# A two-layer graph network on one core: features in place and between the first ticks, the order check later, x over two queues

## The chip, the core and the metric

The kernel runs on one core of a Trainium2 chip. The core has a matrix engine (TensorE, PE in the profile, with its weight loads as PEld), a vector engine (VectorE, DVE), a scalar engine (ScalarE, ACT), a general engine (GpSimd, POOL) and a queue engine (SyncE, SP). Each takes its own instructions in order; they meet through semaphores. DMA transfers are issued by SP, ACT or POOL and run beside the engines. The metric is the device time of one execution in microseconds, as a median of several runs.

## The reference, cut to what matters

There are N = 12500 nodes with 64 features and E = 200000 edges from `src` to `dst`, with `dst` sorted. Two blocks follow each other, both with a residual:

```
h  = relu(layernorm(x))
h1 = relu(mean over edges into v of h[src]  @ W1l.T + b1 + h  @ W1r.T)
x2 = x + (mean over edges into v of h1[src] @ W2l.T + b2 + h1 @ W2r.T)

h  = relu(layernorm(x2))
m  = relu(concat(h[src], h[dst], edge_attr) @ LW1 + lb1) @ LW2 + lb2
out = x2 + mean of m over the edges that leave v
```

The two means of the first block are called the first and the second convolution below; the second block is the message stage.

## The kernel before, in words

**Blocks and cells.** The nodes are cut into 49 blocks of 256 (128 partitions, two nodes each). The edges of one block of destinations are a window of `dst`; within it they are sorted by the block of their source into 49 cells of up to 128 edges. So there are 49 x 49 = 2401 cells. A convolution goes through all cells in order, four at a time; one such step is called a tick below. For a cell PE gathers source features with a one-hot matrix (`got`, L890), ACT copies them to SBUF as bf16 (`rows`, L894), and PE adds them up by destination with a second one-hot matrix (`acc`, L769). DVE makes the one-hot matrices: `turned` (L735) from the row `srow`, two halves for each part of 16 cells, and `hot` (L744) from columns, one for each tick. Features are kept as three bf16 terms whose sum is the f32 number: table `ta` for the first convolution, `tb` for the second.

**Sorting.** `sort(B)` (L589 to L663) ranks the edges of block B on DVE, PE and ACT. It writes the rows `srow_b`, `srow_k` and `drow_k` to DRAM and columns to SBUF; it has 13 steps. `srow` is loaded back from `srow_b`, one part at a time, two parts ahead (L725). `edges_in` loads `src` and `dst` of the next blocks (`ids_i`, L545), from places in `begin_i`, which `find_blocks` has computed.

**The block search.** `find_blocks` (L18 to L109) loads all of `dst` as 125 rows of 1600 (`find_d`), checks that `dst` is in order (L33 to L42, L105 to L109: each number against its neighbour, with two small loads `find_n` for the neighbours at the ends of rows), shifts the numbers to block numbers (L47, L50) and counts where each block begins. The iota `find_ids_i` (L53) is made by POOL, behind the copy `seen` (L699), which waits for the last chunk of x, and the clearing of the end of `tb` (L700). `bad` gets 1 where the fast path can't be used; it is copied to `which` (L959) when the first convolution has been written out in the program, and a general path runs at the end if it is 1.

**Features.** x is loaded into the space of `tb` in seven chunks of seven blocks, by ACT's queue (L203, L208). `features` (L470 to L497) makes `ta` from them: for each chunk two reductions, a subtraction of the mean, a reciprocal and a multiplication on DVE (`layernorm_relu`, L325 to L338), Square, Sqrt, Relu and two copies on ACT, two subtractions on POOL (L348, L352). Its scratch (`h1`, `ln_sq`, `three_r` and statistics) is in a pool of its own, "in". The chunks are begun one after the other, two ticks of a `Line` apart, each tick one step of every chunk under way. After each tick `others` makes two steps of the block search, one of the sorter and one of the clearing. Only when all seven chunks, the search and the first block's sort are written out do the pools of the first convolution open.

**Clearing.** The tables `terms` in DRAM must be zero before edge terms are scattered into them. `zeros` (L272 to L284) issues one such transfer of zeros at each call, on SP: 52 for the first four tables (48 of 640 KB), then smaller ones for the others. In the first convolution a call is made for so many cells as the generator says (5 for the first four tables).

**Beside the convolutions.** From cell 150 on `edge_terms` (L357 to L427) multiplies edge features with weights, and POOL scatters them into `terms` (L385).

**What sets the order.** The program is written in the order in which it is to be run: each generator's step appends its instructions to the engines' queues, and each engine works them off in that order.

## Time and profile before

| what | value |
| --- | --- |
| three runs, median | 3682.99 us (3680.9 to 3687.05) |
| profiled execution | 3679.43 us |
| its span | 3677.6 us |
| granted clock of TensorE, mean | 0.988 |
| first `turned` of the first convolution | 89.7 us |
| last instructions of the first convolution, `which` copied | 1307.4 us |
| DVE instructions L735, L744 in the whole span | 777.6 + 320.2 us and 807.5 us |
| POOL scatters L385 | 1904.0 us, 1666 of 1143 ns |

The page gives, for each engine, busy time and share of the span. A window gives the same for a stretch. In a timeline a row is the start in us, the length in us, engine, line, operation, output and inputs; in square brackets is how long the engine had stood idle before it and what ended that. In the chain of waits each step is what released the one after it; "issue" is time in which the engine waited for nothing that the profile shows. SPq, ACTq and DVEq are the engines' queues, with the DMAs that they issue.

### The profile page before, as it was taken

Reading aid. Unit: us, or ns where it says so; the run is one execution under the profiler, and the core shown is the slowest. Engines: PE = TensorE matmul, PEld = TensorE weight load, DVE = VectorE, ACT = ScalarE, POOL = GpSimd, SP = SyncE. Lnnn points to the kernel's source line nnn. Section 1 sums busy time; section 2 is a strip of 40 time slices with the busy share of each in tenths; the row PEclk is TensorE's granted clock in tenths of the full one; section 3 lists DMA queues with packets and bytes.
Section 4 is the critical chain, followed back from the end, with each engine's and each line's share of the span. In section 5 each row is a group of like instructions: output and inputs, shape, how many; then the busy total and the mean of one; then the engine's idle time right before and its main releaser. Section 6 shows DMA issues by size and latency. Waiting matters only on the chain.

```text
span 3677.6 us, 126942 instructions
## 1 busy us (share of the span) xinstructions
PE 3425.8 (93%) x50925; PEld 3367.7 (92%) x50925; DVE 3269.0 (89%) x5738; ACT 2506.9 (68%) x5949; POOL 2698.3 (73%) x2305
## 2 busy tenths in 40 slices
PE   1799999999899999999999998999999999999987
PEld 0788989898889999999999997999999999999887
DVE  7999999999999978788788787899889998998998
ACT  3455656565556667777777775788888888887665
POOL 4067787777777877777777773788888888887444
PEclk9999999999999999999999999999999999999999
DMA  6754545554454434444444444666766666666664
GB/s 211 268 164 150 169 152 163 155 161 151 147 168 145 128 125 142 132 137 147 136 131 137 140 134 144 224 214 200 218 212 211 204 214 214 207 207 206 194 211 140
DMA packets 413671, 635.66 MB, mean 173 GB/s; under 512 B 94131, under 2 KB 296247, under 8 KB 413070
## 3 DMA queue, kind: packets, MB, share of 16 engines
q1 hardware_dynamic: 353106, 572.87, 49.4%
q0 software_dynamic: 53312, 51.36, 4.1%
q8 instruction: 399, 6.54, 0.7%
q10 hardware_dynamic: 6652, 3.24, 0.4%
q14 instruction: 202, 1.65, 0.1%
HBM read 474.72 MB, written 155.83 MB: 171 GB/s over the span
## 4 chain that ended last, share of the span: by engine, by line
PE 64%; DVE 25%; DMA 5%; issue 3%; POOL 2%; SPq 1%; ACT 1%; DVEq 0%; ACTq 0%; POOLq 0%
PE acc L769 23%; PE got L890 13%; PE got L1071 12%; PE got L1072 6%; DVE hot L744 6%; DVE turned L735 4%; PE pE L417 3%; DVE hot_r L629 3%; PE pE L402 2%; DVE ranks L617 1%; DVE turned_d L735 1%; POOL terms L385 1%; DMA terms<-tb 1%; DMA terms_in<-terms 1%; DVE hot L594 1%
## 5 line engine op out<-in xcount | busy, mean ns | idle before, releaser
L385 POOL DMA_INDIRECT terms<-terms_o,turn_i x1666 | 1904.0, 1143 | 649.9 <-issue 427.8
L894 ACT CAST rows<-got 128x384 bf16<-128x384 f32 x2402 | 1038.4, 485 | 657.2 <-PE got L890 642.6
L769 PEld LDWEIGHTS <-hot 128*128 128x128 bf16 x12006 | 1032.5, 99 | 13.5 <-issue 4.0
L769 PE MATMUL acc<-rows,hot 128*128 128x193 bf16 x9604 | 1010.8, 248 | 0.0
L1083 POOL TENSOR_TENSOR hidden<-hidden 128x512 f32<-128x512 f32 (+1 forms) x602 | 756.4, 1256 | 265.1 <-ACT hidden L1080 179.5
L890 PEld LDWEIGHTS <-turned 128*128 128x128 bf16 x9604 | 814.6, 98 | 88.1 <-DVE turned L735 58.9
L744 DVE TENSOR_TENSOR hot<-dcol,local 128x1024 bf16<-128x1024 bf16 x1202 | 807.5, 682 | 9.0 <-PE acc L769 8.1
L735 DVE TENSOR_SCALAR turned<-srow,nid 128x2048 bf16<-128x2048 bf16 (+1 forms) x906 | 777.6, 872 | 20.7 <-issue 10.6
L1071 PE MATMUL got<-ta,turned 128*128 128x128 bf16 x3920 | 600.1, 221 | 7.3 <-DVE turned L735 7.3
L1071 PE MATMUL got<-tb,turned_d 128*128 128x128 bf16 x3920 | 600.6, 221 | 1.1 <-DVE turned_d L735 0.8
L890 PE MATMUL got<-ta,turned 128*128 128x192 bf16 x4802 | 510.5, 249 | 71.5 <-DVE turned L735 47.9
L1072 PE MATMUL got<-tb,turned_d 128*128 128x64 bf16 x3920 | 546.3, 193 | 0.0
L1072 PE MATMUL got<-ta,turned 128*128 128x64 bf16 x3920 | 546.1, 193 | 0.0
L1091 ACT ACTIVATE hot_a<-every,scol 128x256 bf16<-128x256 bf16 x1200 | 507.0, 493 | 0.0
L890 PE MATMUL got<-tb,turned 128*128 128x192 bf16 x4802 | 494.4, 246 | 0.9 <-DVE turned L735 0.5
L1080 ACT ACTIVATE hidden<-y 128x512 f32<-128x512 f32 (+1 forms) x301 | 190.4, 633 | 272.5 <-DVE y L1077 156.2
L1071 PEld LDWEIGHTS <-turned 128*128 128x128 bf16 x3920 | 362.1, 98 | 8.2 <-issue 7.8
L1071 PEld LDWEIGHTS <-turned_d 128*128 128x128 bf16 x3920 | 359.5, 98 | 1.7 <-DVE turned_d L735 1.7
L1072 PEld LDWEIGHTS <-turned 128*128 128x128 bf16 x3920 | 359.4, 98 | 1.2
L1072 PEld LDWEIGHTS <-turned_d 128*128 128x128 bf16 x3920 | 359.9, 98 | 0.0
L1093 ACT ACTIVATE hot_a<-hot_a 128x1024 bf16<-128x1024 bf16 x300 | 317.2, 1057 | 9.5
L735 DVE TENSOR_SCALAR turned_d<-drow,nid 128x2048 bf16<-128x2048 bf16 (+2 forms) x302 | 320.2, 1101 | 0.0
(217 smaller groups left out, 4898.1 us busy)
## 6 DMA issues: line engine op xcount, KB each, us to landing
srow<-srow_b SPq DMA_DIRECT2D x300, 512.0 KB
srow<-srow_k SPq DMA_DIRECT2D x149, 512.0 KB
drow<-drow_k SPq DMA_DIRECT2D x149, 512.0 KB
terms_in<-terms SPq DMA_DIRECT2D x294, 160.0 KB
edges<-in_edge_attr_dram SPq DMA_DIRECT2D x200, 192.0 KB
terms<-tb SPq DMA_DIRECT2D x200, 160.0 KB
terms<-tb SPq DMA_DIRECT2D x48, 640.0 KB
terms<-terms_o,turn_i POOLq DMA_INDIRECT x1666
```

Of the source, the lines that this page charges most:

```text
L385: nc.gpsimd.indirect_dma_start(out=terms[j][:], out_offset=bass.IndirectOffsetOnAxis(ap=at[:, c, h:h + 1], axis=0), in_=o[:, c, h], in_off ...
L735: nc.vector.tensor_scalar(o[:, h, :n * S], r[:, :n * S], nid[:, h:h + 1], None, op0=OP.is_equal)
L744: nc.vector.tensor_tensor(o[:, :n], cols.rearrange("p (g c) -> p g c", c=2).unsqueeze(2).to_broadcast([P, n, 2 * P, 2]), local.rearrange(" ...
L769: nc.tensor.matmul(self.acc[B][:, h, :W3], lt, r[:, c, 0:W3], start=k + h == 0, stop=k == row - 1 and h == 1, skip_group_check=True)
L890: nc.tensor.matmul(p[:, (i - c) * D3:(i - c + 1) * D3], t[:, h, (a - c0 + i) * S:(a - c0 + i + 1) * S], table[:, (a + i) % NB, h], start=h ...
L894: nc.scalar.copy(g[:, c:c + m, :D3], p[:, :m * D3].rearrange("p (c d) -> p c d", c=m))
L1071: nc.tensor.matmul(p[:, c], lt, rt[:, 0:2 * D], start=i == 0, stop=False, skip_group_check=True)
L1072: nc.tensor.matmul(p[:, c, 0:D], lt, rt[:, 2 * D:], start=False, stop=i == 3, skip_group_check=True)
L1080: nc.scalar.activation(w[:, :n, 0:D], y[:, :n], AF.Relu)
L1083: nc.gpsimd.tensor_sub(w[:, :n, (i + 1) * D:(i + 2) * D], w[:, :n, j], upper(w)[:, :n, j])
L1091: nc.scalar.activation(q[:, c - k], every, AF.Abs, scale=-1.0, bias=scol[:, scol_at[last] + a + c:scol_at[last] + a + c + 1])
L1093: nc.scalar.activation(q[:, :n - k], q[:, :n - k], AF.Relu, bias=1.0, scale=-2.0)
```

## The change

1. `features` works in place: the chunk itself (in the space of `tb`) takes mean, scale, Relu and the remainder of the first term, and the scratch for squares and statistics is a buffer named `edges` of the pool "terms", which is used for edge features only later. The pool "in" is gone.
2. `features` is a generator. The loop ahead of the first convolution ends as soon as the search is done, the first block is sorted and chunk 0 is finished. What is left of the other chunks is taken up between the ticks of the first convolution: one step of the line at each tick, and more where the cells five ahead need a chunk that isn't finished.
3. The order check leaves `find_blocks`. `order_check` loads `dst` again, once more as rows of 1600 with one number of the next row behind, and compares in the first ticks of the second convolution; `which` is copied after it.
4. Of the seven chunks of x the first two are loaded by ACT, the other five by SP, right behind `find_d`.

The diff, with lines of no weight left out:

```diff
@@ find_blocks
-    n = work.tile([R, 2], I32, name="find_n")
-    rows = dst.rearrange("(r c) -> r c", c=C)
-    nc.vector.memset(n, 0)
-    nc.sync.dma_start(n[0:R - 1, 0:1], rows[0:R - 1, C - 1:C])
-    nc.sync.dma_start(n[0:R - 1, 1:2], rows[1:R, 0:1])
     yield
-    down = work.tile([R, C], BF, name="find_down")
-    nc.vector.tensor_tensor(down[:, 0:C - 1], d[:, 0:C - 1], d[:, 1:C], op=OP.is_gt)
-    nc.vector.tensor_tensor(down[:, C - 1:C], n[:, 0:1], n[:, 1:2], op=OP.is_gt)
+    nc.vector.tensor_scalar(d, d, blk.bit_length() - 1, None, op0=OP.arith_shift_right)
     yield
-    flags = work.tile([R, 1], FT, name="find_flags")
-    nc.vector.tensor_reduce(flags, down, AX.X, OP.max)
-    yield
-    q = d
-    nc.vector.tensor_scalar(q, d, blk.bit_length() - 1, None, op0=OP.arith_shift_right)
-    yield
-    qb = down
-    nc.vector.tensor_copy(qb, q)
+    q = work.tile([R, C], BF, name="find_q")
+    nc.vector.tensor_copy(q, d)
+    first = work.tile([R, 1], FT, name="find_first")
+    nc.vector.tensor_copy(first, d[:, 0:1])
...
-    pf = psum.tile([1, P], FT, name="find_pf")
-    nc.tensor.transpose(pf[:, :R], flags, ident[:R, :R])
+
+def order_check(tc, work, psum, ident, bad, dst):
+    nc = tc.nc
+    R = 125
+    C = dst.shape[0] // R
+    rows = dst.rearrange("(r c) -> r c", c=C)
+    d = work.tile([R, C + 1], I32, name="order_d")
+    nc.vector.memset(d[96:R, C:], 2 ** 30)
+    nc.sync.dma_start(d[:, 0:C], rows)
+    nc.sync.dma_start(d[0:R - 1, C:], rows[1:R, 0:1])
+    for _ in range(4):
+        yield
+    down = work.tile([R, C], BF, name="order_down")
+    nc.vector.tensor_tensor(down[:, 0:C // 2], d[:, 0:C // 2], d[:, 1:C // 2 + 1], op=OP.is_gt)
     yield
-    f = work.tile([1, 1], FT, name="find_f")
-    nc.vector.tensor_reduce(f, pf[:, :R], AX.X, OP.max)
+    nc.vector.tensor_tensor(down[:, C // 2:], d[:, C // 2:C], d[:, C // 2 + 1:], op=OP.is_gt)
+    yield
+    for k in (C // 2, C // 4):
+        nc.vector.tensor_max(down[:, 0:k], down[:, 0:k], down[:, k:2 * k])
+    yield
+    flags = work.tile([R, 1], FT, name="order_flags")
+    nc.vector.tensor_reduce(flags, down[:, 0:C // 4], AX.X, OP.max)
+    yield
+    p = psum.tile([P, 512], FT, name="pX")
+    nc.tensor.transpose(p[0:1, :R], flags, ident[:R, :R])
+    yield
+    f = work.tile([1, 1], FT, name="order_f")
+    nc.vector.tensor_reduce(f, p[0:1, :R], AX.X, OP.max)
     nc.vector.tensor_max(bad, bad, f)
@@ fast_path, loads of x
-    for s, xs in enumerate(xs_all):
+    for s, xs in list(enumerate(xs_all))[:2]:
         full = min((s + 1) * CH, FULL) - s * CH
         nc.scalar.dma_start(
...
     next(finding)
+    for s, xs in list(enumerate(xs_all))[2:]:
+        full = min((s + 1) * CH, FULL) - s * CH
+        nc.sync.dma_start(
+            xs[:, :full],
+            x[s * CH * BLK:(s * CH + full) * BLK].rearrange("(b p h) d -> p b h d", p=P, h=2))
+        if full < CH:
+            nc.vector.memset(xs[96:P, full], 0.0)
+            nc.sync.dma_start(xs[:REST // 2, full], x[FULL * BLK:N].rearrange("(p h) d -> p h d", h=2))
@@ features
+    featured = set()
+
     def features():
-        def some(work, s):
-            h = work.tile([P, 2 * CH, D], FT, name="h1", bufs=2)
-            xs = xs_all[s].rearrange("p b h d -> p (b h) d")
-            yield from layernorm_relu(work, h, xs, 2 * CH, xs)
-            yield from three(work, ta[:, s * CH:(s + 1) * CH].rearrange("p b h d -> p (b h) d"), h,
-                             nc.gpsimd.tensor_sub)
...
-        with tc.tile_pool(name="in", bufs=3, side="right") as work:
-            line = Line()
-            for s in range(NB // CH):
-                line.tick(some(work, s))
-                others()
-                line.tick()
-                others()
-            while line.all:
-                line.tick()
-                others()
-            while not found[0] or sorted_to[0] < STEPS:
-                others()
+        def some(s):
+            n = 2 * CH
+            v = xs_all[s].rearrange("p b h d -> p (b h) d")
+            o = ta[:, s * CH:(s + 1) * CH].rearrange("p b h d -> p (b h) d")
+            room = terms_work.tile([P, 12, 2 * D], FT, name="edges").rearrange("p c d -> p (c d)")
+            sq = room[:, :n * D].rearrange("p (n d) -> p n d", d=D)
+            st = room[:, n * D:n * D + 3 * n].rearrange("p (k n) -> p k n", k=3)
+            nc.vector.tensor_reduce(st[:, 0], v, AX.X, OP.add)
+            nc.vector.scalar_tensor_tensor(v, bc(st[:, 0], D), -1.0 / D, v, op0=OP.mult, op1=OP.add)
+            yield
+            nc.scalar.activation(sq, v, AF.Square)
+            yield
+            nc.vector.tensor_reduce(st[:, 1], sq, AX.X, OP.add)
+            yield
+            nc.scalar.activation(st[:, 2], st[:, 1], AF.Sqrt, bias=small, scale=1.0 / D)
+            yield
+            nc.vector.reciprocal(st[:, 1], st[:, 2])
+            nc.vector.tensor_mul(v, v, bc(st[:, 1], D))
+            yield
+            nc.scalar.activation(v, v, AF.Relu)
+            nc.scalar.copy(o[:, :, 0:D], v)
+            yield
+            nc.gpsimd.tensor_sub(v, v, o[:, :, 0:D])
+            yield
+            nc.scalar.copy(o[:, :, D:2 * D], v)
+            yield
+            nc.gpsimd.tensor_sub(o[:, :, 2 * D:], v, o[:, :, D:2 * D])
+            featured.add(s)
+
+        line = Line()
+        for s in range(NB // CH):
+            line.tick(some(s))
+            yield
+            line.tick()
+            yield
+        while line.all:
+            line.tick()
+            yield
...
-    features()
+    coming_features = features()
+    while not found[0] or sorted_to[0] < STEPS or 0 not in featured:
+        next(coming_features, None)
+        others()
@@ the ticks of the convolutions
         for a, z in part:
+            if layer == 0:
+                next(coming_features, None)
+                while min(z + 5, NB - 1) // CH not in featured:
+                    next(coming_features)
             line.tick_behind(some_cells(layer, t, c0, a, z))
...
             if layer:
+                if ordered is not None and next(ordered, ordered) is ordered:
+                    ordered = None
+                    ordering.close()
+                    nc.vector.tensor_copy(which, bad)
                 gathered[0] = max(z - (CELLS - NB), 0)
                 again()
         if layer == 0 and c1 == CELLS:
...
-            nc.vector.tensor_copy(which, bad)
             sorting.close()
+            ordering = ExitStack()
+            ordered = order_check(tc, ordering.enter_context(tc.tile_pool(name="order", bufs=1, side="right")),
+                                  psum_x, ident, bad, dst)
```

More of the change, by code (lines that the diff above doesn't have):

```diff
@@ L59, in find_blocks @@
     nc.vector.tensor_copy(own, own_i)
-    first = work.tile([R, 1], FT, name="find_first")
-    nc.vector.tensor_copy(first, q[:, 0:1])
     less = work.tile([R, nb], FT, name="find_less")
@@ L77, in find_blocks @@
         pr = psum.tile([nb, F], FT, name="find_pr", bufs=2)
-        nc.tensor.matmul(pr, pick, qb[:, k:k + F], start=True, stop=True)
+        nc.tensor.matmul(pr, pick, q[:, k:k + F], start=True, stop=True)
         nc.vector.tensor_scalar(row[:, k:k + F], pr, own[:nb], None, op0=OP.is_lt)
@@ L205, in fast_path @@
             x[s * CH * BLK:(s * CH + full) * BLK].rearrange("(b p h) d -> p b h d", p=P, h=2))
-        if full < CH:
-            nc.vector.memset(xs[96:P, full], 0.0)
-            nc.scalar.dma_start(xs[:REST // 2, full], x[FULL * BLK:N].rearrange("(p h) d -> p h d", h=2))
     raw_in = first.enter_context(tc.tile_pool(name="raw", bufs=1))
@@ L468, in finish @@
                 self.tick()
+    featured = set()
     def features():
-        def some(work, s):
-            h = work.tile([P, 2 * CH, D], FT, name="h1", bufs=2)
-            xs = xs_all[s].rearrange("p b h d -> p (b h) d")
-            yield from layernorm_relu(work, h, xs, 2 * CH, xs)
-            yield from three(work, ta[:, s * CH:(s + 1) * CH].rearrange("p b h d -> p (b h) d"), h,
-                             nc.gpsimd.tensor_sub)
-        def others():
-            for _ in range(2):
-                if next(finding, found) is found:
-                    found[0] = True
-            if sorted_to[0] < STEPS:
-                next(sorter)
-            next(clearing, None)
@@ L499, in fast_path, with others @@
+        line = Line()
[7 more added lines that the diff above has]
+            yield
+    def others():
+        for _ in range(2):
+            if next(finding, found) is found:
+                found[0] = True
+        if sorted_to[0] < STEPS:
+            next(sorter)
+        next(clearing, None)
     found = [False]
```

## The prediction

> **What bounds the kernel now.** I read the busy times first, then the windows by stage, then the chain of waits and the timeline of the first 110 us, where all but one part of the change lies.
>
> ```profile
> PE 3425.8 (93%) x50925; PEld 3367.7 (92%) x50925; DVE 3269.0 (89%) x5738; ACT 2506.9 (68%) x5949; POOL 2698.3 (73%) x2305
> ```
>
> Over the whole span PE looks like the bound. The windows (length, then busy time and instructions of PE, PEld, DVE, ACT and POOL, granted clock, DMA share, GB/s) say which engine it is in each stage:
>
> ```profile
> 12.00:14.00 2.00, 0.00 (x0) 0.00 (x0) 0.81 (x1) 0.00 (x0) 0.00 (x0) 1.00 0.42 108
> 20.00:22.00 2.00, 1.55 (x17) 1.33 (x16) 1.97 (x3) 1.97 (x3) 0.00 (x0) 1.00 1.23 268
> 60.00:80.00 20.00, 1.27 (x11) 0.83 (x8) 17.76 (x18) 12.65 (x20) 13.37 (x7) 1.00 0.92 346
> 80.00:100.00 20.00, 4.45 (x33) 3.55 (x33) 10.07 (x21) 3.71 (x6) 4.89 (x8) 1.00 0.64 228
> 400.00:600.00 200.00, 186.12 (x2285) 180.72 (x2284) 196.72 (x375) 121.15 (x327) 162.26 (x124) 1.00 0.51 159
> 1320.00:1360.00 40.00, 40.00 (x460) 39.74 (x458) 29.13 (x59) 27.27 (x71) 31.29 (x29) 1.00 0.43 140
> ```
>
> Before the first gather (0 to 90 us) DVE does nearly all of the work. In the first convolution (to 1307 us) it is still DVE: 196.72 of 200 us, PE 186.12. In the second, PE is full and DVE has 11 us free in 40. So a microsecond of DVE saved or lost before about 1260 us, when the sorting ends, reaches the end of the kernel; one of PE counts after that. The chain shows where DVE stands still:
>
> ```profile
> 74.15 1.88 POOL ta L352
> ...
> 79.03 0.13 DVE wcat L708
> 79.16 10.46 issue
> ...
> 89.72 0.13 DVE turned L735
> ```
>
> The timeline names the cause:
>
> ```profile
> 23.46 0.18 POOL L699 COPY seen<-tb 1x1 f32<-1x1 f32 x1 [19.02 <-DMA tb<-in_x_dram]
> 24.91 0.17 POOL L53 IOTA find_ids_i<- 125x49 int32 x1
> 25.67 0.28 DVE L55 CAST find_ids<-find_ids_i 125x49 f32<-125x49 int32 x1
> 55.15 2.82 POOL L348 TENSOR_TENSOR three_r<-h,ta 128x896 f32<-128x896 f32 x1 [4.60 <-ACT ta L346]
> 56.15 2.90 DVE L629 TENSOR_TENSOR hot_r<-rank_b,rexp 128x2048 bf16<-128x2048 bf16 x1
> 83.86 1.88 POOL L352 TENSOR_TENSOR ta<-three_r,ta 128x896 bf16<-128x896 f32 x1 [1.05 <-ACT ta L350]
> 85.76 5.72 SPq L725 DMA_DIRECT2D srow<-srow_b  x3
> 104.32 1.22 DVE L629 TENSOR_TENSOR hot_r<-rank_b,rexp 128x2048 bf16<-128x2048 bf16 x1
> ```
>
> The first `srow` load goes out at 85.76, when the last feature subtraction ends at 85.74: its buffer lies where the features' pool was. DVE waits 10.56 us for it. Two more things are to be seen: the copy `seen` waits for the last chunk of x, and the iota that the block search needs stands behind it; and a DVE instruction that meets a POOL subtraction is stretched (2.90 us against 1.22 alone).
>
> **The change, part by part.** All terms are DVE time up to the sorting's end unless said otherwise. They are added to the profiled execution: 3679.43 us, its span 3677.6 and 1.8 around it, 3.6 under the median of 3682.99. I add the same sum to the median.
>
> *Order check leaves the start.* L33, L38, L39, L42, L108, L109: 0.06 + 1.82 + 0.15 + 1.82 + 0.27 + 0.15 = **-4.3**. The shift and the cast of `find_d` (0.99 each) stay.
>
> *Features in place.* The seven chunks keep their DVE instructions (1.08 + 1.09 + 1.08 + 0.23 + 1.09 each). All of them but the last two reciprocals, two multiplications and one reduction still stand before the first `turned`, because the loop must turn 13 times for the first block's sort; the five (3.7 us) move behind it. DVE is full on both sides, so the move itself is 0. What changes is the waits.
>
> *The wait of 10.56 goes*, since the scratch now lies in the `edges` buffers and no longer under `srow`: **-10.6**. Late next is `srow` itself. From the end of chunk 5's subtraction of the mean (64.89) to `rows_o` took 2.15 us; then the row's write (I take the 2.27 of a scatter's landing in the chain) and the load (3.9, from 85.76 to 89.62): 8.4. Beside it DVE has L644 and L645 0.4, reciprocal, multiplication, two reductions, subtraction 4.6, L554, L555 and `wcat` 1.0, and one stretched by 1.7: 7.7. One clear (0.64 MB, 1.9 us at the 346 GB/s of the window at 60) lies between write and load. Ends 0 and 4; I take **+1.5**.
>
> *The iota becomes a wait.* DVE now reaches the cast of `find_ids` at 18.4: 13.19 + 1.1 + 1.0 (chunk 0) + 0.9 + 0.9 + 0.1 (shift, cast, first) + 1.0 (L594). The iota ended at 25.1, 1.6 after `seen` got its chunk. If x lands as now, the wait is 6.7. If x and dst (4.0 MB) move at the 301 GB/s of the best window of the first 24 us from 4 us on, the chunk is there at 17.3 and the wait 0.5. From 18 to 22 us the DMA share was 1.2, so the transfer engines finished late, not ACT's queue; hence nearer the late end: **+5**. Loading x from SP as well takes 12 us of issue from ACT's queue, so the first Square can run at 15.4 rather than 20.7; that gains 0, since its reader L333 waited for DVE, not for ACT. The weights, now behind x on SP, are first read at 66.65, 36 us after they land at the latest. The Trainium skill ("DMA: Bandwidth & Descriptors", Issuing engines are not separate DMA queues) says that a second issuing engine saves only issue time; by that the chunk lands as now and the wait is the full 6.7, which makes the sum 1.7 worse.
>
> *The last chunk's square root* stands on ACT behind the second block's `cols_o`, four copies and a Relu: 1.3 for PE's 16 products, 0.6, and three times 0.95 make some 5 us after the second half of L629, while DVE asks for the root after 3.2 us of other work: 0 to 3, **+2**.
>
> *Subtractions against DVE.* Stretched in the first 80 us: L338 4.2 in all (1.53, 1.41, 1.30), L629 1.68, L644 1.69, L97 1.45, L624 0.99, L612 0.6: 10.6 for 14 subtractions, of which four met reductions or an idle DVE and cost nothing. After the change about nine such meetings fall before the gather with 9 us in all (7 to 11), and five subtractions fall in the ticks, where DVE runs almost only `turned`, `hot` and sort instructions. Dearest: 1.88 each, 9.4. Cheapest: the message stage, where L735 takes 1.09 against 0.75 beside 450 subtractions, 0.34 each, 1.7. I take four at 1.88, as in the start, since the fifth falls into the wait for the root: 7.5. Net 9 + 7.5 - 10.6 = **+5.9** (-2 to +9.8). The Trainium skill ("SBUF — State Buffer", Who interferes with whom) says that an instruction of DVE with two SBUF inputs and a POOL instruction that reads SBUF exclude each other for the whole instruction. That agrees with 2.90 against 1.22 and speaks against the move: by it all five cost 1.88, the sum 1.9 worse; by the message stage it is 5.8 better.
>
> *Clears.* The loop calls the clearing 14 times instead of 23, so the 640 KB clears last 9 x 5 = 45 cells longer (23 us at 0.507 a cell), beside the first edge loads at cell 150. From 140 to 200 us, where they now end, DVE lacked 3.5 us in 60: **+1.3**, ends 0 and 5. POOL's first scatter now comes right behind its clears; three `terms_o` buffers cover it.
>
> *Order check in the second convolution.* Two comparisons of half width (0.91 each), two maxima (about 0.8), a reduction (0.46), three small ones (0.6): 3.7 on DVE, under 11 free in 40. The 800 KB load and its 124 single numbers share DMA at 0.43; SP's early read of the flag now waits some 7 ticks, with `srow` loads that are two parts ahead behind it. PE's transposition of the flags, 0.37, is on the path: **+0.4** (0 to 3.7).
>
> **Sum**: -4.3 - 10.6 + 1.5 + 5 + 2 + 5.9 + 1.3 + 0.4 = **+1.2 us**: 3680.6 for the profiled execution, **3684** for the median. The ends add up to -16.5 and +17.2.
>
> **Rivals.** *Faster: the ticks swallow the features.* If subtractions cost 0.34 in the ticks (-5.8) and x lands early enough for an iota wait of 1.5 (-3.5): -8, 3675. For it: 10.56 us of plain idle is removed and PE has 7% free to catch up. Against: DVE ran 29.5 of 30 us from 90 to 120.
>
> *Slower: clears in front of the first row.* Five clears stand on SP between the `ids_i` loads and the row's write; each moves 1.9 us. Now the `ids_i` loads took 10.7 us (48.64 to 59.3) after `begin_i`; I expect `begin_i` at 42, the clears at 53, drained by 63, the write at 70. If that margin of 7 is used up, `srow` waits for up to 9.5 more: +10.7, 3694. It decides from a row wait of 8 us.
>
> *No change of the start:* if another buffer of the `layers` pool still waits for the last subtraction, the 10.6 stay and the moved subtractions only add: about +8 to +10, 3692. Against: the scratch has another pool; only the search and the weights lie under `srow`.
>
> **How the numbers follow.** A measurement of this kernel can tell about 0.2%, 7.4 us, from no change. No change 0.40, faster 0.33 (its first rival, and any two terms near their low ends), slower 0.27 (the two other rivals, or the lock at full price with the iota at 6.7). The range takes in the ends of the terms but for a tenth on each side: 3669 to 3698; for the likeliest case alone 3677 to 3690.
>
> **What would show it.** First `turned` at 77 us (74 to 81) instead of 89.72; a DVE wait of about 5 us for POOL's iota at 18 to 24 us; a wait for ACT's root between 95 and 105; sort or `turned` instructions of 2 to 3 us beside subtractions between 85 and 110; conversion from first to second convolution at 1308 (1295 to 1322) instead of 1307; the order check with PE unbroken. The forecast is wrong if the first `turned` comes at 77 but the gain of 12 us is still there at 150 us, or if DVE is idle before `turned` for more than 8.

## The result and the profile after

The changed kernel takes 3696.47 us (median of six runs, 3694.7 to 3704.4) where the kernel before takes 3684.69 (six runs, 3677.48 to 3687.99): a ratio of 1.0039, with a 95% interval from 1.0029 to 1.0050 (the two medians alone give 1.0032). It is slower, by some 12 to 14 us. The forecast was no change at 3684; the time lies inside its range of 3669 to 3698, but not inside the likeliest case's own, 3677 to 3690.

The profiled execution of the changed kernel took 3700.0 us, its span 3698.2, 3.5 above its own median; the one of the kernel before was 5.3 below the median of its six runs. So the two traces lie 20.6 us apart, more than the medians. Busy times, on the page of the changed kernel:

```profile
PE 3437.2 (93%) x50925; PEld 3379.3 (91%) x50925; DVE 3278.7 (89%) x5740; ACT 2506.6 (68%) x5949; POOL 2707.0 (73%) x2305
```

Its windows, with the columns as before (length, busy times of PE, PEld, DVE, ACT, POOL, granted clock, DMA share, GB/s):

```profile
12.00:14.00 2.00, 0.00 (x0) 0.00 (x0) 0.54 (x4) 0.00 (x0) 0.00 (x0) 1.00 1.21 270
20.00:22.00 2.00, 0.00 (x0) 0.00 (x0) 0.62 (x1) 0.00 (x0) 0.00 (x0) 1.00 0.52 139
60.00:80.00 20.00, 2.97 (x24) 2.29 (x25) 19.31 (x21) 9.45 (x15) 11.47 (x10) 1.00 0.55 184
80.00:100.00 20.00, 8.18 (x74) 6.89 (x72) 18.51 (x35) 4.73 (x10) 1.47 (x1) 0.74 0.28 93
400.00:600.00 200.00, 183.64 (x2227) 178.65 (x2226) 192.94 (x368) 117.12 (x317) 160.45 (x129) 0.98 0.51 154
1320.00:1360.00 40.00, 35.85 (x376) 34.78 (x375) 29.22 (x60) 23.12 (x58) 29.63 (x27) 0.91 0.45 134
```

The stretch from 80 to 100 us, where DVE had been idle for half of the time, is now 18.51 busy. From 1320 to 1360, where PE had been full, it now lacks 4.15.

The start went nearly as forecast. The chain of waits no longer has a stretch of 10 us of "issue"; DVE comes to `turned` as the row lands:

```profile
72.30 5.60 DMA srow<-srow_b
...
78.03 1.42 DVE turned L771 x2
```

The timeline of the changed kernel shows the waits that were to come in its place:

```profile
22.82 0.18 POOL L732 COPY seen<-tb 1x1 f32<-1x1 f32 x1 [18.38 <-DMA tb<-in_x_dram]
24.46 0.26 DVE L42 CAST find_ids<-find_ids_i 125x49 f32<-125x49 int32 x1 [3.84 <-POOL find_ids_i L40]
78.03 1.42 DVE L771 TENSOR_SCALAR turned<-srow,nid 128x2048 bf16<-128x2048 bf16 x2 [0.48 <-DMA srow<-srow_b]
100.51 0.24 DVE L501 RECIPROCAL edges<-edges 128x14 f32<-128x14 f32 x1 [1.61 <-ACT edges L499]
100.78 2.65 DVE L502 TENSOR_TENSOR tb<-tb,edges 128x896 f32<-128x896 f32 x1
106.22 2.72 DVE L645 TENSOR_TENSOR hot<-hot,dlo 128x1666 bf16<-128x1666 bf16 x1
```

The wait for the iota is 3.84, the one for the row 0.48, the one for the root 1.61, and a DVE instruction beside one of POOL's subtractions takes 2.65 where it took 1.09.

**Where the time went.** To see when the lag arises, I set the 9604 products that gather features (L890 before, L926 after) side by side, the nth of one trace against the nth of the other. The lag of the changed kernel, at the moment at which the kernel before starts that product:

| at, us | 98 | 123 | 135 | 150 | 180 | 190 | 240 | 450 | 900 | 1240 | 1300 | 1340 | 2240 |
| --- | --- | --- | --- | --- | --- | --- | --- | --- | --- | --- | --- | --- | --- |
| lag, us | -12.2 | +1.3 | -0.4 | +2.7 | +1.2 | +9.8 | +8.3 | +7.9 | +7.7 | +9.4 | +16.7 | +21.4 | +21.7 |

At 135 us all that the start gains and loses is through, and the sum is -0.4. The forecast's terms up to there, without the 1.3 for the clears and the 0.4 for the second convolution, are -0.5. Then come three steps: 8.7 between 135 and 240 us, some 7 around 1250 to 1290, and 4.7 at 1310. The first, in the timeline of the changed kernel:

```profile
147.49 0.75 DVE L771 TENSOR_SCALAR turned<-srow,nid 128x2048 bf16<-128x2048 bf16 x1 [2.85 <-DMA srow<-srow_b]
...
179.88 3.96 SPq L291 DMA_DIRECT2D terms<-tb  x3
...
185.78 10.03 SPq L381 DMA_DIRECT2D edges<-in_edge_attr_dram  x8
...
191.99 0.97 PE L414 MATMUL pE<-ident,edges 128*128 128x128 f32 x2 [6.29 <-DMA edges<-in_edge_attr_dram]
...
195.92 0.37 SPq L761 DMA_DIRECT2D srow<-srow_b  x1
```

and in that of the kernel before:

```profile
180.70 8.19 SPq L369 DMA_DIRECT2D edges<-in_edge_attr_dram  x8
...
184.74 0.33 PE L402 MATMUL pE<-ident,edges 128*128 128x128 f32 x1 [0.26 <-DMA edges<-in_edge_attr_dram]
...
189.00 0.37 SPq L725 DMA_DIRECT2D srow<-srow_b  x1
```

The first edge features are issued behind 640 KB clears that in the kernel before were out by then. PE has its place in the order for them and waits 6.29 us, where it waited 0.26; the row load behind them goes out 6.9 us later. The windows of the changed kernel show the same as DMA share, and DVE with 67.9 us of work in 80, where the kernel before had 76.2:

```profile
140.00:160.00 20.00, 15.51 (x178) 14.89 (x176) 16.87 (x35) 9.29 (x25) 0.00 (x0) 0.91 1.00 360
160.00:180.00 20.00, 14.47 (x176) 13.60 (x174) 18.58 (x43) 8.39 (x24) 0.00 (x0) 0.91 0.85 320
180.00:200.00 20.00, 13.06 (x115) 11.61 (x113) 16.51 (x32) 6.90 (x17) 0.00 (x0) 0.74 0.90 294
200.00:220.00 20.00, 19.85 (x252) 19.57 (x250) 15.94 (x29) 12.49 (x36) 7.90 (x7) 1.00 0.65 217
```

The last step stands right behind the order check's load. Timeline of the changed kernel:

```profile
1324.04 0.36 SPq L99 DMA_DIRECT2D order_d<-in_dst_dram  x1
...
1331.46 0.97 POOL L397 DMA_INDIRECT terms<-terms_o,turn_i  x1 [2.33 <-DMA terms<-terms_o,turn_i]
1332.19 0.58 ACT L437 COPY terms_o<-pE 128x512 f32<-128x512 f32 x1 [3.30 <-DMA terms<-terms_o,turn_i]
...
1332.83 1.12 PE L414 MATMUL pE<-ident,edges 128*128 128x128 f32 x4 [3.29 <-ACT terms_o L437]
...
1333.95 0.29 DVE L852 TENSOR_TENSOR both<-sums 128x128 f32<-128x128 f32 x1 [4.49 <-ACT sums L846]
...
1335.89 0.99 DVE L104 TENSOR_TENSOR order_down<-order_d 125x800 bf16<-125x800 int32 x1
```

Read from the bottom: the check's first comparison comes at 1335.89, when the damage is done. Before it, with the load under way, POOL's scatters don't land, so ACT has no free buffer of `terms_o` (3.30), so PE has no bank for the next edge features (3.29), and DVE waits 4.49 for ACT. The same products and the same sum in the run without the check, which is described below:

```profile
1322.99 0.66 PE L414 MATMUL pE<-ident,edges 128*128 128x128 f32 x4
...
1324.12 0.29 DVE L852 TENSOR_TENSOR both<-sums 128x128 f32<-128x128 f32 x1 [1.10 <-ACT sums L846]
```

The transfers in the trace of the changed kernel show when the load moves: its 125 rows of 6.4 KB from 1327 to 1335 us, 16 to 20 of them in each microsecond from 1330 to 1334, most of them 0.24 us long. That is the time of 4 to 5 of the 16 transfer engines (an estimate from these numbers). Packets of the rows `srow` lie beside them until 1330. The 124 single numbers of the check follow at 1334 to 1336, too late to cause these waits.

The middle step also is a chain of waits for scatters, but nothing of the change is near it; the experiments show what it is worth.

In three of the five comparisons below (their runs are marked *) every kernel, the one before included, took 20 to 23% longer, from 200 us on, so their traces are read up to 200 us only, and their ratios have wide intervals.

### The profile page after: what moved, and what is told of

It reads as the page before. It is cut to its first block, busy times and chain, and to the rows that moved or that the text cites. A ratio compares the mean times of both kernels' runs of the same rounds, so it can differ in the third digit from the quotient of the medians.

```text
span 3698.2 us, 126955 instructions
## 1 busy us (share of the span) xinstructions
PE 3437.2 (93%) x50925; PEld 3379.3 (91%) x50925; DVE 3278.7 (89%) x5740; ACT 2506.6 (68%) x5949; POOL 2707.0 (73%) x2305
## 4 chain that ended last, share of the span: by engine, by line
PE 64%; DVE 21%; DMA 5%; issue 4%; SPq 2%; POOL 2%; ACT 1%; DVEq 0%; POOLq 0%; ACTq 0%
PE acc L805 23%; PE got L926 13%; PE got L1117 12%; PE got L1118 6%; DVE hot L780 5%; DVE turned L771 4%; PE pE L429 4%; DVE hot_r L662 2%; POOL terms L397 2%; PE pE L414 2%; DVE turned_d L771 1%; DVE ranks L650 1%; DMA terms_in<-terms 1%; DMA terms<-terms_o,turn_i 1%; PE got L1114 1%
## 5 line engine op out<-in xcount | busy, mean ns | idle before, releaser
L926 PEld LDWEIGHTS <-turned 128*128 128x128 bf16 x9604 | 819.6, 98 | 65.8 <-DVE turned L771 51.9
L780 DVE TENSOR_TENSOR hot<-dcol,local 128x1024 bf16<-128x1024 bf16 x1202 | 811.2, 685 | 10.8 <-PE acc L805 10.0
L926 PE MATMUL got<-ta,turned 128*128 128x192 bf16 x4802 | 514.2, 250 | 49.4 <-DVE turned L771 41.1
L926 PE MATMUL got<-tb,turned 128*128 128x192 bf16 x4802 | 495.7, 247 | 0.9 <-DVE turned L771 0.9
```

The costliest lines, as they stand in the source:

```text
L780: nc.vector.tensor_tensor(o[:, :n], cols.rearrange("p (g c) -> p g c", c=2).unsqueeze(2).to_broadcast([P, n, 2 * P, 2]), local.rearrange(" ...
L926: nc.tensor.matmul(p[:, (i - c) * D3:(i - c + 1) * D3], t[:, h, (a - c0 + i) * S:(a - c0 + i + 1) * S], table[:, (a + i) % NB, h], start=h ...
```

## The experiments

"Clears" are the 640 KB transfers of zeros on SP. The lag is always against the first profile of the kernel before, by the same products; the step is the lag at 1340 less that at 1300. The diffs leave out lines that only set up or switch the names used in them. Three profiles of the changed kernel agree within 0.2 us at 135 and lie at +7.5 to +9.0 at 200; three of the mended version below within 0.4 at 135 and at -3.0 to -5.4 at 200.

**Clears, from both sides.** Nine clears put back into the changed kernel (54 stand before the first edge load then, 53 in the kernel before, 45 in the changed one):

```diff
@@ others, called in each turn of the loop ahead of the convolution
         next(clearing, None)
+        if turns[0] < 4:
+            next(clearing, None)
+        turns[0] += 1
@@ ticks of the first convolution
+                if a == 0:
+                    for _ in range(5):
+                        next(clearing)
                 while filled < z:
```

> The changed kernel with nine more clears of the message tables early: a second one in each of the first four turns of the loop ahead of the convolution, and five in its first tick, behind the first three row loads, where the DMA share was 0.00 (90 to 100 us). So 54 clears stand before the first edge load, as many as before (53), not 45. Theory of the clears: the changed kernel is 0.37 us ahead at 123 us and 8.3 behind at 235, because clears stand between the edge loads and the rows at 180 to 210 us; with them gone the lag at 235 us is within 2 of nothing, and the time is 8 to 12 below the changed kernel's 3696.5: 3685 to 3689. Rival, the order check in the second convolution (12 us more lag between 1220 and 1340 us): the lag at 235 may go, but the 12 remain, 3688 to 3692 if it is real in every execution. Rival, subtractions that meet DVE: no change, 3694 to 3698.

Measured: the lag at 240 us is +2.4 where it was +8.3 (2 at most was expected), and POOL's first scatter comes 6.0 us earlier. PE no longer waits at the first edge features:

```profile
186.89 0.29 PE L414 MATMUL pE<-ident,edges 128*128 128x128 f32 x1
```

Its windows where the changed kernel lost most:

```profile
180.00:200.00 20.00, 17.60 (x218) 16.78 (x216) 19.69 (x40) 9.98 (x25) 0.00 (x0) 1.00 0.67 188
200.00:220.00 20.00, 19.82 (x245) 19.36 (x241) 19.47 (x38) 13.24 (x36) 14.01 (x12) 1.00 0.46 143
```

DVE has 19.69 and 19.47 of 20 there (16.51 and 15.94 without the edit). Ratio 1.0014 (1.0002 to 1.0026), against the changed kernel's 1.0039 from another comparison: some 9 us less. That lies in the 8 to 12 expected, but each interval is some 4 us wide on either side, and the trace gives 6. The wait for the row at 147 us stays (lag at 150: +3.5), and so do 3.0 us between 135 and 240.

The same term, alone, in the kernel before:

```diff
@@ features, others
-            next(clearing, None)
+            if turns[0] < 14:
+                next(clearing, None)
+            turns[0] += 1
```

> The kernel before with one thing alone of the change: 14 clears instead of 23 in the features' stage, so 45 before the first edge load. Theory of the clears: it loses what the changed kernel lost, 8 to 12 us: 3692 to 3697 where the kernel before has 3684.7, with the loss between 140 and 235 us; POOL's first scatter 8 to 10 us later. Rivals (order check, subtractions): within 3 us of the kernel before, 3682 to 3688. My own prediction's size of the term was 1.3 (0 to 5).

Measured, with 46 clears before the first edge load: level to 0.7 us up to 180, then +6.8 at 240, by the same wait:

```profile
184.10 9.99 SPq L369 DMA_DIRECT2D edges<-in_edge_attr_dram  x8
190.31 0.18 PEld L402 LDWEIGHTS pE<-ident,edges 128*128 128x128 f32 x1 [6.46 <-DMA edges<-in_edge_attr_dram]
```

Ratio 1.0013 (0.9998 to 1.0028). So nine clears that end 45 cells later cost 6 to 7 us at 180 to 240, shown from both sides by the traces. The times agree in sign but are too coarse for the size; the interval of the second just includes no change. At the row of 147 us this kernel loses nothing (lag at 150: 0.0).

**The order check left out.**

```diff
             sorting.close()
-            ordering = ExitStack()
-            ordered = order_check(tc, ...)
+            nc.vector.tensor_copy(which, bad)
+            ordered = None
```

> The changed kernel without the order check: its load of dst, comparisons, maxima and transposition are left out, and the flag is copied at the end of the first convolution, as before. This part of the computation is missing. Theory of the clears: the check costs next to nothing, 3694 to 3697 against 3696.5. Rival, the order check costs the 12 us of lag that appear between 1220 and 1340 us: 3684 to 3686, and the lag stays at 9 behind 1340 us.

Measured: lag +8.4 at 240 as in the changed kernel, +8.6 at 1300 and +8.6 at 1340: neither the step at 1310 nor the one around 1270. The ratio, 1.0032 (1.0018 to 1.0046), doesn't show a gain; its profiled execution was the shortest of twelve. So the step of 4.7 is shown by the traces, and the time neither confirms nor excludes it. The run leaves out the whole check; that its load is the part that costs follows from the order in the trace above, where the waits of POOL, ACT, PE and DVE all end before the first comparison.

**The iota in front of `seen`,** on top of the nine clears:

```diff
@@ find_blocks, ahead of the load of find_d
+    ids_i = work.tile([R, nb], I32, name="find_ids_i")
+    nc.gpsimd.iota(ids_i, pattern=[[1, nb]], base=0, channel_multiplier=0)
+    own_i = work.tile([R, 1], I32, name="find_own_i")
+    nc.gpsimd.iota(own_i, pattern=[[0, 1]], base=0, channel_multiplier=1)
```

> The kernel of the nine clears put back, and besides the two iotas of the block search ahead of the copy that waits for the last chunk of x. In the changed kernel DVE waited 3.84 us for the iota at 20.6 to 24.5 us. If DVE's start is what the end follows: 3 to 4 us below the kernel with the clears alone, 3681 to 3686, below the kernel before by a little. If POOL's scatters set the end of the first convolution and their start is set by the clears: within 1.5 of the kernel with the clears alone.

Measured: no wait is left before the cast, the lag is -4.6 at 135 us and -2.9 at 240, against -0.6 and +2.4 without the edit; ratio 0.9996 (0.9984 to 1.0008). All of the 4.0 that it wins at the start is kept to the end of the clears, and 1.3 more.

**More clears sooner, edges sooner, x by one queue\*.** All three start from the kernel with clears and iota mended. The first two have ten clears in the first tick instead of five; the second also `a >= 140` for `a >= 150` where the edge terms begin; the third has five clears there, and `nc.scalar` for `nc.sync` in the five loads of x. Beside them the changed kernel again.

> As the kernel with nine clears and the iotas in front, with ten clears in the first tick instead of five, so the last 640 KB clear is out some 25 cells earlier. The DMA share was 0.00 at 90 to 100 us and 0.38 to 0.48 at 110 to 130, and 0.85 to 1.00 from 140 to 200. Theory of the clears (what counts is how long they stand between rows and edge loads): the lag at 240 us goes from -2.9 to -5 or -8, the time 2 to 5 us below that kernel's ratio of 0.9996: 0.998 to 0.999. If the rows of the second and third block (101 us) are held up by them, the lag at 123 us grows instead, by up to 5 us. Rival, POOL's scatters wait for nothing but their own time: no change at 240 us.

> The kernel with ten clears in the first tick, with the edge terms begun at cell 140 instead of 150, some 5 us earlier, and so that many more of them done in the first convolution. POOL is without a gap there (162 of 200 us busy, 34 more in the gaps of 0.3 us ahead of each scatter, waits 5). If POOL's start sets the end of the first convolution: 3 to 5 us faster than without this edit. If DVE alone bounds it (196.7 of 200): no change within 2, or 1 to 3 slower, since the same work on PE comes earlier while the rows still fill the DMA.

> The kernel with nine clears and the iotas in front, with all seven chunks of x loaded by ACT, as before the change. In the changed kernel the first subtraction of the mean came 2.3 us later than before (15.48 against 13.19 us), beside five more chunks that SP issues. If chunk 0 shares the transfer engines with them: the start 1 to 2.3 us earlier, the lag at 135 us -6 to -7 instead of -4.6, the time 1 to 2 lower. Rival, SP is 5 us busy longer without effect and ACT's queue is the one that counts: ACT's first Square moves from 15.4 back to 20.7, and since no subtraction of features stands before it, its reader waits up to 3 us: 1 to 3 slower.

> The changed kernel once more, unaltered, so that its variants are compared on the same chip. The kernel before ran from 3681 to 3699 in the earlier comparison, so a single execution varies by 9 us either way. Lag behind the kernel before at 240 us as in its first profile, 8.3 within 1; time 12 to 15 us over the kernel before (1.0032 to 1.0042) if the lag at 240 us is most of the loss and some 3 to 6 come later; 8 over if all that comes later is chance.

Measured up to 200 us: the changed kernel +7.5 (first profile +8.3). Ten clears in the first tick -2.7, no better than five (-2.9), a miss. With five the lag is -3.0 at 180 and -2.9 at 240, so there was nothing left to win at the edge loads; nor were the first rows held up, since the lag at 123 is -2.6 (-2.9 with five). Edges ten cells earlier +7.3, a loss of 10 where a gain, no change or a loss of up to 3 was expected. Of it 2.8 us are there at 150 already, before the edge terms begin. The first edge load is issued when it was without the edit (177.14 against 177.02), and PE waits 2.52 us for it. The lag is +2.5 at 190; the rest up to 200 comes in products of PE for which the trace names no cause. So why this edit costs stays open. x by ACT alone -6.2 at 135 and -5.4 at 200; chunk 0 is there when it was in the kernel before:

```profile
13.21 1.09 DVE L492 TENSOR_REDUCE edges<-tb 128x14 f32<-128x896 f32 x1 [1.35 <-DMA tb<-in_x_dram]
```

In the changed kernel this instruction starts at 15.48. So the second queue costs 2.3 us at the start, of which 1.6 are left at 135.

**The row at 147 us\*.** The kernel with clears and iota mended, without clears between cells 50 and 95 (they are made up for behind):

```diff
-                while filled < z:
+                while filled < z and not 50 < z < 95:
```

> The kernel with nine clears and the iotas in front, whose loop issues no clears between cells 50 and 95 and makes up for them behind. The changed kernel and most variants of it waited 2.9 us for a row load at 147 us (0.8 in the kernel before), issued at 142 behind a clear that held SP for 1.7 us. Theory, the clears on SP hold it up: the wait goes to under 1 us, the lag behind the kernel before stays at -4.6 at 150 us (it went to -1.6 without this edit), and the loss comes behind 170 us instead. Rival, the row comes late because the products of the third block run at the half clock (granted clock 0.50 to 0.75 at 87 to 118 us), which sends SP's whole sequence 1.7 us later against DVE: the wait stays at 1.5 to 3.

Measured: the lag is -5.6 at 150 us, where it was -1.6, and the wait comes back behind the ten clears that were made up for:

```profile
141.11 12.15 SPq L291 DMA_DIRECT2D terms<-tb  x10
...
163.10 0.75 DVE L775 TENSOR_SCALAR turned<-srow,nid 128x2048 bf16<-128x2048 bf16 x1 [4.87 <-DMA srow<-srow_b]
```

So the wait goes when no clears stand ahead of that row, and comes where ten do. But clears ahead of a row are not enough for it: the kernel before has them too, and its wait at this place is short and not for the row:

```profile
145.70 0.75 DVE L735 TENSOR_SCALAR turned<-srow,nid 128x2048 bf16<-128x2048 bf16 x1 [0.77 <-PE acc L833]
```

Why is not settled. Its row load left at 139.72, the changed kernel's at 141.97. Three profiles of one version, all mended, lose 1.1, 2.7 and 4.8 us between 135 and 150.

**Queue or transfer engines?** All mended (nine clears, iotas in front, x by ACT), and then the clears of the first 200 cells issued by another engine:

```diff
-                nc.sync.dma_start(
+                (nc.gpsimd if other[0] else nc.sync).dma_start(
                     terms[j].rearrange...
```

> The version with nine clears put back, the iotas in front and x loaded by ACT alone, a third time, since both comparisons so far had everything, the kernel before included, take 20% longer from 200 us on. At 200 us it was 5.4 and 3.0 us ahead of the kernel before. If that is kept: 0.9985 to 0.9992 of the kernel before; if the later stretches cost whatever the start has done: 1.000 to 1.002.

> The same version, with the clears of the first 200 cells issued by POOL, which is idle from 80 to 200 us, and not by SP. If the clears cost time because rows and edge loads stand behind them on SP's queue: no wait of DVE for a row above 1 us between 130 and 200 us, and the lag at 200 us goes from -3 or -5 to -6 or -7. If the transfer engines are the limit (share 0.95 to 1.03 at 140 to 165 us): the waits stay, and the lag at 200 us is as without the edit or worse, since more clears are then under way beside the rows. The issue by POOL may also stretch DVE: up to 3 us later.

> As the run with POOL, with ACT issuing the clears. ACT was busy 7 to 11 of 20 us from 140 to 200 us, and an issue held SP for 1.0 to 1.7 us where the transfer engines were full: 20 of them would cost ACT 25 us of 120, and PE waits for ACT's copies of rows. If the queue's order is the cause: ahead at 200 us by 5 to 7 as with POOL, less what ACT loses; if ACT's time counts: the lag at 200 us above 0.

Measured: all mended -3.5 at 240 us and 1.0003 (0.9992 to 1.0014), so no gain in time over the kernel before. With POOL +12.9 at 240 and 1.0053 (1.0038 to 1.0067); its rows wait most of all:

```profile
144.61 0.75 DVE L775 TENSOR_SCALAR turned<-srow,nid 128x2048 bf16<-128x2048 bf16 x1 [8.90 <-DMA srow<-srow_b]
...
156.71 0.75 DVE L775 TENSOR_SCALAR turned<-srow,nid 128x2048 bf16<-128x2048 bf16 x1 [6.23 <-DMA srow<-srow_b]
```

and its window shows what goes with it:

```profile
120.00:140.00 20.00, 16.93 (x225) 16.55 (x222) 15.58 (x24) 10.46 (x27) 8.09 (x11) 1.00 1.03 380
```

From 118 to 140 us POOL issues 12 clears where SP had issued 9, and they move at 380 GB/s (243 with SP). So rows wait for clears that are not in their queue; SP's order is not needed for it. These rows agree with the Trainium skill, "DMA: Bandwidth & Descriptors", Issuing engines are not separate DMA queues: all issuers share the same transfer engines.

With ACT -1.4 at 240, no better than SP, but by another way. DVE waits for no row between 120 and 200 us, though the transfer engines are as full; what is lost is lost behind ACT, which stands idle for 5.10 us ahead of its copy at 135.70:

```profile
135.70 0.48 ACT L934 CAST rows<-got 128x384 bf16<-128x384 f32 x1 [5.10 <-DMA ids_i<-in_src_dram]
```

A window of the same run:

```profile
140.00:160.00 20.00, 18.54 (x233) 18.07 (x230) 16.95 (x32) 12.35 (x33) 0.00 (x0) 0.99 1.02 395
```

So a share of 1.0 alone does not tell whether a row will be late. Which of the two, the place in the queue or the moment at which the clears are under way, sets the wait at 147 us is not decided by these runs.

**The kernel before, again, and how far executions drift.**

> The kernel before, profiled a second time, to see how far two executions of the same instructions drift apart. If all lag that appears behind 240 us in the variants is chance: level within 0.5 us up to 240 us, then apart by up to 5 to 12 us by 1340 us. If the changed kernel really loses 12 us around 1250 to 1340 us: the second profile keeps within 3 us of the first throughout.

> The kernel before, profiled a third time. The second kept within 0.15 us of the first up to 200 us, and could not be compared behind that. If the further lags of the variants behind 240 us are chance: it drifts from its first profile by 5 to 12 us by 1340 us. If they belong to the change: it stays within 3.

Measured: within 0.2 us of the first profile up to 200 (the second\*); the third within 0.4 up to 150 and at 240, with +1.3 at 190 between, then -4.4 at 900, +1.8 at 1240, +4.5 at 1300, +5.1 at 1340. So the same instructions drift apart by 5 us either way, in the first convolution, with the three largest jumps (5.2, 2.3 and 1.9 us) at waits of ACT for scatters to land; the step around 1270 in the changed kernel's trace is of this size and has none of the change beside it. It was not settled beyond that.

**The check's load in pieces\*,** in the mended version and in the changed kernel:

```diff
-    nc.sync.dma_start(d[:, 0:C], rows)
+    for k in range(0, C, C // 8):
+        nc.sync.dma_start(d[:, k:k + C // 8], rows[:, k:k + C // 8])
+        yield
```

> The mended version (nine clears put back, iotas in front, x by ACT) with the order check's load of dst in eight pieces of 100 KB, one a tick. If the 800 KB in one piece hold up the scatters: no step of 4 to 5 us at 1310 us, the version stays 3 us ahead there, and its time is 0.9980 to 0.9992 of the kernel before (1.0003 with the load in one piece). If the check costs by its instructions on DVE and PE (3.7 us and 0.4): the step stays, 1.000 to 1.001.

> The changed kernel with that edit alone. If the load in one piece is the cause of the step: about 8 behind the kernel before from 240 us to the end of the second convolution apart from the drift of a single profile, 1.0020 to 1.0030 against 1.0039. If not: 1.0035 to 1.0045, with the step of 4 to 5 us at 1310.

Measured: the step can't be read in these two traces. SP issued the eight pieces within 5.7 and 5.0 us, though the ticks should have spread them. POOL's longest wait behind them was 4.9 and 5.0 us; with the load in one piece it was between 2.4 and 4.9 in the seven other marked runs that have the check. So whether pieces of 800 bytes a row mend it stays open.

Two more repeats\*, whose intervals decide nothing:

> The version with nine clears put back, the iotas in front and x loaded by ACT alone, once more, since in its first comparison everything, the kernel before included, took 20% longer from 200 us on. Up to 200 us it was 5.4 us ahead of the kernel before there. If what is gained at 200 us is kept: 0.9985 of the kernel before, 5 us below it. If the later stretches cost whatever the start has done: 1.000 to 1.002.

> The changed kernel, unaltered, beside the mended version and the kernel before on one chip. Lag at 240 us 8.3 within 1, as in both profiles so far (8.34; 7.46 at 200 us on the other chip). Time: 1.0020 to 1.0045 of the kernel before; if the lag at 240 us were all, 1.0023.

| run | lag at 135 | at 150 | at 200 | at 240 | step at 1310 | ratio to the kernel before |
| --- | --- | --- | --- | --- | --- | --- |
| changed kernel | -0.4 | +2.7 | +8.3 | +8.3 | +4.7 | 1.0039 (1.0029 to 1.0050) |
| changed, again* | -0.5 | +3.8 | +7.5 | | | 1.0007 (0.9975 to 1.0039) |
| changed, third* | -0.5 | +3.2 | +9.0 | | | 1.0016 (0.9980 to 1.0051) |
| clears back | -0.6 | +3.5 | +2.4 | +2.4 | +4.9 | 1.0014 (1.0002 to 1.0026) |
| before, fewer clears | +0.3 | 0.0 | +6.8 | +6.8 | -0.4 | 1.0013 (0.9998 to 1.0028) |
| no order check | -0.7 | +3.5 | +8.3 | +8.4 | 0.0 | 1.0032 (1.0018 to 1.0046) |
| clears, iota | -4.6 | -1.6 | -2.9 | -2.9 | +4.5 | 0.9996 (0.9984 to 1.0008) |
| and ten clears in tick 1* | -4.7 | -2.4 | -2.7 | | | 0.9953 (0.9918 to 0.9988) |
| and edges at cell 140* | -4.7 | +0.4 | +7.3 | | | 0.9958 (0.9924 to 0.9993) |
| all mended* | -6.2 | -5.1 | -5.4 | | | 0.9961 (0.9924 to 0.9998) |
| all mended, again* | -5.8 | -3.1 | -3.0 | | | 0.9984 (0.9947 to 1.0021) |
| all mended, third | -6.2 | -1.4 | -3.5 | -3.5 | +5.2 | 1.0003 (0.9992 to 1.0014) |
| clears by POOL | -3.5 | +12.4 | +13.0 | +12.9 | +5.5 | 1.0053 (1.0038 to 1.0067) |
| clears by ACT | -4.4 | -1.5 | -1.4 | -1.4 | +5.6 | one run, 3685.1 us |
| before, again* | +0.1 | -0.1 | 0.0 | | | one run, 4528.6 us |
| before, third | +0.1 | -0.4 | -0.2 | -0.2 | +0.6 | one run, 3685.9 us |
| no clears, cells 50 to 95* | -4.9 | -5.6 | -0.7 | | | one run, 4509.3 us |
| mended, pieces* | -6.8 | -5.7 | -6.2 | | | 0.9980 (0.9942 to 1.0017) |
| changed, pieces* | -0.3 | +4.7 | +9.9 | | | 1.0011 (0.9976 to 1.0046) |

The column of the step settles the order check: six traces that have it lose 4.5 to 5.6 us there, three that don't lose 0.6 at most. Lag at 240 and step together give the ratio: for the mended version -3.5 + 5.2 = 1.7 us or 0.0005, measured 0.0003; for the clears by POOL 18.4 us or 0.0050, measured 0.0053; for the changed kernel 13.0 us or 0.0035, measured 0.0039. The other four unmarked ratios have the sum inside their intervals as well: 0.0020 for the clears put back (0.0014), 0.0017 for fewer clears (0.0013), 0.0023 without the check (0.0032), 0.0004 with the iota (-0.0004). The three marked ratios whose intervals lie below 1 are of kernels that stand at -2.7, +7.3 and -5.4 at 200 us, so they don't follow from the start, and no unmarked run shows a version that beats the kernel before.

## Why the prediction was wrong, point by point

- *What bounds the kernel*, and that DVE's time till the sorting's end counts in full: right as far as it was tried. The iota's 4.0 us at 135 were still there at 240, and so were the clears' 6.
- *Order check leaves the start, wait of 10.56 goes, `srow` +1.5, iota +5, root +2, subtractions +5.9:* the sum holds, -0.4 against -0.5 at 135 us, and the first `turned` at 78.03 against 77. The terms: the row's wait 0.48, the iota's 3.84, the root's 1.61, the stretched instructions in the ticks 6.6 to 6.8 (L502, L645 and L780 by 1.6 to 1.7 each and one of L650) against 7.5. Seven instructions of DVE ahead of the first `turned` (L82, L502 twice, L587, L650, L662, L677) are stretched by 1.4 to 1.7, in all 11.1 against 9. One term was missing: chunk 0 of x landed 2.3 us later beside the five loads of the second queue, and this is also why the iota's wait came out below 5. That the sum agrees to 0.1 is luck: four terms came out 3.4 us too high, two 4.4 too low. Two small sums were off as well, without effect: by their own terms the 18.4 of the cast is 18.2, the 8.4 of the row 8.3. The rule weighed there from the Trainium skill ("DMA: Bandwidth & Descriptors", Issuing engines are not separate DMA queues) held for the last chunk: it was there at 22.82, not at 17.3, against 23.46 before. The rule on DVE and POOL excluding each other ("SBUF — State Buffer", Who interferes with whom) held for four instructions in the ticks, at 1.6 to 1.7 rather than 1.88.
- *Clears +1.3, ends 0 and 5:* this is the step that failed first. Nine clears that end 45 cells later cost 6 to 7 us, from both sides. I had read 3.5 us of missing DVE time from the windows at 140 to 200 of the kernel before, where the clears just make room in time, and scaled that. But the price isn't DVE time lost to a busy DMA; it is what stands behind the clears: the first edge load has its fixed place in PE's order, and PE waits for it whole (6.29 us). "POOL's first scatter now comes right behind its clears; three `terms_o` buffers cover it" looked at the wrong waiter. In the changed kernel's trace the stretch from 135 to 240 us lost 8.7 in all: 3.1 at the row of 147 us, 1.5 of which came back by 180, and 7.1 at the first edge loads. The row's part stays with the nine clears put back and doesn't come in the kernel before with nine fewer, so it isn't this term's; the prediction had no term for it, and its cause is open.
- *Order check in the second convolution +0.4, ends 0 and 3.7:* measured 4.7, and 4.5 to 5.6 in six traces. Its instructions are as cheap as forecast (0.99, 0.99, 0.57, 0.42, 0.56 on DVE). Its load isn't: "share DMA at 0.43" took the mean share for room. Scatters land late beside the 800 KB, and through `terms_o` they stop ACT, PE and DVE at once. "PE unbroken" was broken for 3.29 us.
- *The end of the first convolution* came at 1323, not in 1295 to 1322. The check hasn't begun there; the 8.3 us of the start and the step around 1270 make it so.
- *Rivals:* none of the three happened. The one with clears in front of the first row had the right culprit at the wrong place: the first row waited 0.48, while a later row and the edge loads paid.

-0.4 + 8.7 + 4.7 = 13.0 us, against 11.8 between the medians and 14 by the ratio. The other 7 or 8 of the 20.6 between the two profiled executions are of the size of the drift.

## What to carry to other kernels

When early work is taken out of a loop, count what else the loop gave a place to: here nine background transfers lost theirs and moved to where the transfers were already full. Cost a transfer that moves not by its share of the DMA but by the first instruction behind it that can't start without its own data, on whichever engine that is. A mean DMA share of 0.4 was no room here for 800 KB at once, since buffers are freed by small transfers that must land beside them.

## What the runs showed of the hardware

- Three profiles of the kernel before agree within 0.4 us up to 150 us (1.3 at 190); the two that can be compared behind 240 us drift apart by up to 5. Up to 240, matching instructions one by one tells differences that the times can't.
- The granted clock of 1.00 is not to be trusted ahead of a trace's first record of the clock, which in the kernel before stands at 109.5 us. Weight loads of the same line in the kernel before, at a granted clock of 1.00 throughout:

```profile
103.19 1.44 PEld L639 LDWEIGHTS <-hot_r 128*128 128x128 bf16 x18 [5.31 <-DVE hot_r L629]
...
116.98 0.86 PEld L639 LDWEIGHTS <-hot_r 128*128 128x128 bf16 x18 [1.69 <-DVE hot_r L629]
```

and in the changed kernel, at 0.50 during both:

```profile
90.95 1.44 PEld L672 LDWEIGHTS <-hot_r 128*128 128x128 bf16 x18 [5.32 <-DVE hot_r L662]
...
116.61 1.44 PEld L672 LDWEIGHTS <-hot_r 128*128 128x128 bf16 x18 [6.66 <-DVE hot_r L662]
```

Eighteen loads take 1.44 us at the slow rate and 0.86 at the fast one, and the kernel before was at the slow rate at 103 us too. The changed kernel, whose PE stands idle for 6.66 us before the loads at 116.61, is back at the fast rate only from 120 us on. "TensorE: Matmul & The Clock Gate" of the Trainium skill (Part 1) has the slow rate as the state after an idle window; the loads agree with that, and the column of the clock doesn't ahead of its first record.
